# Layer 0's keys and queries of six of eight head pairs by seven block products

## The chip, the cores and the metric

The kernel runs on one core of one Trainium2 chip. The metric is the device time of one execution in microseconds. Five engines are named in what follows: TensorE (PE, matrix multiplications, with its weight loads shown apart as PEld), VectorE (DVE), ScalarE (ACT), GpSimd (POOL) and SyncE (SP, which here only issues transfers). They run side by side, each through its own list of instructions, and wait for one another through semaphores.

## The reference

Everything is in float32. The input x has 2 batches of 512 channels by 64 x 32 = 2048 tokens. Two layers follow one another.

Layer 0 is a softmax attention with 8 heads of 64. The queries and keys see 64 more channels than the values: an embedding of the row and of the column of a token, the same in both batches.

```python
qk_hs = jnp.concatenate([hidden_states, emb], axis=1)    # 512 + 64 channels
q = qk_hs @ Wq
k = qk_hs @ Wk
v = v_hs @ Wv                                            # 512 channels
scores = jnp.einsum('bhqd,bhkd->bhqk', q, k) * scale
o = jnp.einsum('bhqk,bhkd->bhqd', softmax(scores), v)
return o @ Wout + bout + hidden_states
```

Layer 1 normalises, runs a Nyström attention with 256 landmarks, an iterated pseudo-inverse and a convolution of 33 taps over the values, and then a feed-forward block, whose 4-bit weights are unpacked and composed into one 512 x 512 map. Nothing of layer 1 is changed here, but two of its parts are made during layer 0, as told below.

## The kernel before

**Tiles.** Channels lie on the 128 partitions in four chunks (`KC`), tokens in four blocks of 512 (`TB`, `NTB`). Heads are taken in pairs, so a pair's keys are one tile of 128 x 2048, and there are 2 batches x 4 = 8 pairs, written (b, hp). Names ending in `_f` belong to layer 0.

**Making a pair** (`Heads0`, L861). Its work is a Python generator, `units()`, which issues one unit of instructions each time it is advanced. For the queries and for the keys it first makes the embedding terms `e` of the pair, 128 x 2048: in batch 0 one small matmul (`fp`, L889), a copy (`ft`, L891) and one broadcast addition of a row part and a column part (L894; on DVE for the first pair, on POOL for the next three), and then a store to memory (L900). Batch 1 loads what batch 0 stored (L886). Then `project` (L903) takes one block of 512 tokens per unit: four matmuls 128 x 512, one for each chunk of channels, into a PSUM bank (L907), and one DVE addition of bank and `e` into `k` or `q` (L910). Values are another four units, each of sixteen matmuls 128 x 128 and an ACT copy (L955, L962). Two maxima (L943) end the pair. `bank` hands out one of two PSUM banks. All three weight matrices of layer 0 are loaded whole at the start and stay.

**Attention of a pair** (`attention0`, L1063). 64 steps, four blocks of 512 queries by sixteen tiles of 128 keys, are issued in groups of two. A group issues its scores (L1075), the exponentials on ACT (L1083), their running addition into `acc` on DVE (L1093), and the value products of the group before (L1105). Then it may advance the *filler*, the units of the pair that comes next:

```python
            elif due - done >= 2:
                done += advance(filler, min(due - done, 3))
            if beside and i // GROUP % 8 in (1, 3, 5):
                advance(beside)
```

So a filler step has two or three units, and stands every three to five groups. `beside` is the making of the feed-forward map: DVE unpacks the 4-bit weights (L1169, L1170), a few operations per advance, and PE multiplies at its end. At the end of a query block follow the row sums `rs` (L781), a reciprocal on DVE (L1120), eight small transfers on SP that spread it over partitions (L792), and a multiplication on POOL (L1123).

**Order.** All of layer 0 is written out by the loop at L1806: while the attention of pair n runs, pair n+1 is made. The first pair is made alone at the start. During the attention of (1,0), one unit after every group, stands also `finish0_units`, the output projection of batch 0 (`yp`, L970), its residual (L977), and the statistics of the normalisation (`mean_n` L992, `xn_f` L993, `var_n` L1008); pair (1,1), made there, gets its queries only when the projection is through. Each engine works through its list in the order written. There is no planner.

**Layer 1** already makes its keys and queries by seven block products: `Combined` (L1217) forms differences of token blocks (`t_first`, `t_second`, L1232), `combine_w` those of the weights (L1296), `product` (L1873) issues two matmuls of 128 x 512, and additions from PSUM (L1883) put the blocks together. One bank, `pu`, accumulates over several products and is read in between.

Of the kernel before, what the change touches and what calls it, by code (L numbers as in the profile page):

```python
# [10 lines left out]
F32 = mybir.dt.float32  # L11
I32 = mybir.dt.int32
AF = mybir.ActivationFunctionType
ALU = mybir.AluOpType
AX = mybir.AxisListType

P = 128
B, C, H, W = 2, 512, 64, 32
# [647 lines left out]
def fast_path(  # L666
# [63 lines left out]
    def chunked(ap):  # L730
        return ap.rearrange("(k p) n -> p k n", p=P)

    def bank(name):
        return ps.tile([P, 512], F32, tag="pp", name=name)
# [74 lines left out]
    def drain(gen):  # L809
        for _ in gen:  # L810
            pass

    def gap(n=1):
        for _ in range(n):
            yield GAP
# [7 lines left out]
    emb_sb = wpool0.tile([64, H + W], F32, name="emb_f")  # L823
    nc.vector.memset(emb_sb[:32, H:], 0.0)
    nc.vector.memset(emb_sb[32:, :H], 0.0)
    w_sb = {kind: wpool0.tile([P, KC, C], F32, name=f"w{kind}_f") for kind in "qk"}
    we = {kind: wpool0.tile([64, C], F32, name=f"we{kind}_f") for kind in "qk"}

    def load_w0(kind, cols, queue=nc.sync):
        w = {"q": wq0, "k": wk0}[kind]  # L830
        queue.dma_start(w_sb[kind][:, :, cols], chunked(w[:C, cols]))
        queue.dma_start(we[kind][:, cols], w[C:, cols])

    load_w0("q", slice(0, P), nc.scalar)
    nc.scalar.dma_start(emb_sb[:32, :H], freq)
    nc.scalar.dma_start(emb_sb[32:, H:], time)

# [11 lines left out]
    warm = bank("warm")  # L849
    for i in range(20):  # L850
        nc.tensor.matmul(warm[:, :P], lhsT=mean_w, rhs=mean_w, start=True, stop=True)
    load_w0("k", slice(0, P))
    xbs += load_x(x, 0, "x0", 1, NTB - 1)
    wv_sb = wpool0.tile([P, KC, C], F32, name="wv_f")
    nc.sync.dma_start(wv_sb[:, :, :P], chunked(wv0[:, :P]))
    nc.sync.dma_start(wv_sb[:, :, P:], chunked(wv0[:, P:]))
    for kind in "qk":
        load_w0(kind, slice(P, C))
    nc.sync.dma_start(b0_sb, b0)

    class Heads0:  # L861


        def __init__(self, b, hp, xbs):
            self.b, self.hp, self.xbs = b, hp, xbs
            self.name = f"f0_{b}_{hp}"
            self.n_units = 13 if b else 15

        def begin(self):
            self.cols = slice(self.hp * P, (self.hp + 1) * P)  # L870
            self.k = kvpool.tile([P, S], F32, tag="k", name=f"k_{self.name}")
            self.v = kvpool.tile([P, NST, P], F32, tag="v", name=f"v_{self.name}")

        def embedded_and_projected(self, kind):

            cols, xbs = self.cols, self.xbs
            if kind == "q":
                self.q = qopool.tile([P, S], F32, tag="qo", name=f"q_{self.name}")

            def embedded(kind):  # L880


                e = wpool0.tile([P, H, W], F32, tag="e", name=f"e_{kind}_{self.name}")
                flat, kept = e.rearrange("p h w -> p (h w)"), e_d["qk".index(kind), self.hp]
                if self.b:
                    nc.sync.dma_start(flat, kept)  # L886
                    return flat
                fp = bank(f"fp_{kind}_{self.name}")
                nc.tensor.matmul(fp[:, : H + W], lhsT=we[kind][:, cols], rhs=emb_sb, start=True, stop=True)  # L889
                ft = wpool0.tile([P, H + W], F32, tag="ft", name=f"ft_{kind}_{self.name}")  # L890
                nc.vector.tensor_copy(ft, fp[:, : H + W])  # L891

                engine = nc.gpsimd if self.b or self.hp else nc.vector
                engine.tensor_tensor(  # L894
                    e,
                    ft[:, :H].unsqueeze(2).to_broadcast([P, H, W]),
                    ft[:, H:].unsqueeze(1).to_broadcast([P, H, W]),
                    ALU.add,
                )
                nc.sync.dma_start(kept, flat)  # L900
                return flat

            def project(kind, dst, e, t):  # L903
                toks = slice(t * TB, (t + 1) * TB)
                pp = bank(f"pp_{kind}_{self.name}_{t}")
                for k in range(KC):
                    nc.tensor.matmul(  # L907
                        pp, lhsT=w_sb[kind][:, k, cols], rhs=xbs[t][:, k, :], start=k == 0, stop=k == KC - 1
                    )
                nc.vector.tensor_tensor(dst[:, toks], pp, e[:, toks], ALU.add)  # L910

            dst = self.q if kind == "q" else self.k
            e = embedded(kind)
            if self.b:
                yield from gap(2)
            else:
                yield
                yield GAP
            for t in range(NTB):
                project(kind, dst, e, t)  # L920
                yield

        def values(self):
            for t in range(NTB):
                values_of_tokens(self.v, t, self.xbs[t], lambda k: wv_sb[:, k, self.cols], self.name)
                yield

        def units(self, queries_first=True, ready=None, wait=0):

            self.begin()  # L930
            yield from gap(wait)
            if queries_first:
                yield from self.embedded_and_projected("q")
            yield from self.embedded_and_projected("k")
            yield from self.values()
            if not queries_first:
                while not ready():
                    yield GAP
                yield from self.embedded_and_projected("q")

            big = small.tile([P, 2], F32, tag="big0", name=f"big_{self.name}")
            for i, m in enumerate((self.q, self.k)):
                nc.vector.tensor_reduce(big[:, i : i + 1], m, AX.X, ALU.max, apply_absolute_value=True)  # L943
            i = self.b * NPAIR + self.hp
            nc.vector.scalar_tensor_tensor(
                bound[:, i : i + 1], big[:, :1], D**-0.5, big[:, 1:], ALU.mult, ALU.mult
            )
            yield
# [114 lines left out]
    def attention0(hd, filler, n_filler, needed, beside=None, every=False):  # L1063
# [58 lines left out]
            spread(rinv, few)  # L1122
            nc.gpsimd.tensor_tensor(o, o, rinv, ALU.mult)  # L1123

        pending, done = [], 0
        for i in range(0, len(steps) + 1, GROUP):
            group = [(step, scores(*step)) for step in steps[i : i + GROUP]]
            for step, p in group:
                add(step, p)
            for step, p, its_acc in pending:  # L1130
                values(step, p, its_acc)
            pending = [(step, p, acc) for step, p in group]
            due = n_filler * (i + GROUP) // len(steps)
            if every:
                done += advance(filler, 2 if due - done >= 2 else 1)
            elif due - done >= 2:
                done += advance(filler, min(due - done, 3))
            if beside and i // GROUP % 8 in (1, 3, 5):
                advance(beside)
            if not group:  # L1140
                while needed in filler:
                    advance(filler)
            if late:
                sums(*late)
                late = None
# [658 lines left out]


    todo = [(b, hp) for b in range(B) for hp in range(NPAIR)]  # L1806
    cur = Heads0(0, 0, xbs)
    drain(cur.units())
    ffn_map = [feed_forward_map()]
    oTs, finish, work = [], None, []  # L1810
    for n, (b, hp) in enumerate(todo[:-1]):
        nb, nhp = todo[n + 1]
        if nb != b:
            xbs = load_x(x, nb, "x0")
        nxt = Heads0(nb, nhp, xbs)
        n_fill = nxt.n_units + 2 * len(work)
        if finish is None:
            units = nxt.units(wait=nb - b)
        else:

            units = nxt.units(False, lambda: outs_done)
            work.append(finish)
            n_fill += N_FINISH0
        work.append(units)
        attention0(cur, work, n_fill, units, ffn_map if finish is None else None, finish is not None)
        finish = None
        oTs.append(cur.q)
        if n == 3:
            while ffn_map:
                advance(ffn_map)  # L1830
            wo_sb = load_wo(wo0, "wo_f0")
            write_bands()
        if hp == NPAIR - 1:
            outs_done = []
            finish = finish0_units(b, oTs, outs_done)
            oTs = []
        cur = nxt
# [16 lines left out]
    class Unit:  # L1854
# [15 lines left out]
        def product(self, to, m, start=True):  # L1870
            w, x = self.pair.ws[m], self.part.of[m]
            for k in range(2):
                nc.tensor.matmul(  # L1873
                    to, lhsT=w[:, k, :], rhs=x[:, k, :], start=start and k == 0, stop=k == 1, skip_group_check=True
                )
# [586 lines left out]
```

## Time and profile before

| | |
|---|---|
| median of 3 runs | 2720.01 us (2719.69 to 2721.13) |
| the profiled execution | 2717.38 us, of which the span of the core's work is 2715.6 |
| mean granted PE clock | 0.998 of full |
| PE busy | 2669.3 us, 98% of the span |
| PE weight loads (beside the matmuls) | 1353.2 us, 50% |
| DVE busy | 1676.7 us, 62% |
| ACT busy | 905.5 us, 33% |
| POOL busy | 161.4 us, 6% |
| layer 0's part | about the first half of the span |

Busy time is the time in which an engine executes; an engine that waits for a semaphore is idle, and the trace names who released it. Line numbers are those of the kernel's file. In the groups of the page, a name with `_f` is layer 0's, and the columns are busy time, mean duration of one instruction, and the idle time just before such instructions.

### The profile page before, as it was taken

How to read it: one execution, taken by the hardware profiler on the slowest of the kernel's cores; microseconds unless marked ns; L12 is line 12 of the kernel's file. 1: busy time of each engine (PE TensorE's matmuls, PEld its weight loads, DVE VectorE, ACT ScalarE, POOL GpSimd, SP SyncE). 2: the span in 40 equal slices, each digit the busy share in tenths (PEclk: the TensorE clock that was granted, in tenths of full speed). 3: DMA queues.
4: the chain of work that ended last, by engine and by line, in shares of the span. 5: the costliest groups of instructions: out<-in, count | busy, mean ns of one | idle time of the engine just before them, and what ended most of it. 6: DMA issues, size and time to landing. Idle time of an engine off the chain costs nothing.

```text
span 2715.6 us, 41051 instructions
## 1 busy us (share of the span) xinstructions
PE 2669.3 (98%) x16946; PEld 1353.2 (50%) x16946; DVE 1676.7 (62%) x2115; ACT 905.5 (33%) x1354; POOL 161.4 (6%) x109
## 2 busy tenths in 40 slices
PE   9999999999999999999999899999999999999998
PEld 5343343434443334344344455777677666655344
DVE  3768777674657765656668865535644645465565
ACT  1434344433334334444422323223323223231210
POOL 0101011000001100000001000000000000000000
PEclk9999999999999999999999999999999999999999
DMA  4100000212111300012015632313111113021211
GB/s 148 43 10 24 24 24 24 85 37 70 32 51 58 110 23 22 24 40 77 21 43 180 240 115 102 107 34 107 63 38 62 59 44 101 31 74 39 90 39 48
DMA packets 108021, 174.00 MB, mean 64 GB/s; under 512 B 15792, under 2 KB 67504, under 8 KB 103216
## 3 DMA queue, kind: packets, MB, share of 16 engines
q1 hardware_dynamic: 101680, 150.00, 16.9%
q0 software_dynamic: 5440, 20.97, 2.1%
q8 instruction: 135, 2.21, 0.3%
q14 instruction: 62, 0.51, 0.1%
q10 hardware_dynamic: 704, 0.31, 0.0%
HBM read 90.87 MB, written 63.57 MB: 57 GB/s over the span
## 4 chain that ended last, share of the span: by engine, by line
PE 90%; DVE 6%; ACT 1%; DMA 1%; SPq 1%; issue 1%; POOL 0%; DVEq 0%; ACTq 0%; POOLq 0%
PE sc_f L1075 15%; PE av_f L1105 15%; PE pa L1624 5%; PE pb L1624 5%; PE vp_f L955 4%; PE vp L955 4%; PE pp_k_f L907 4%; PE fp_g L1780 4%; PE yp_g L970 4%; PE yp_f L970 3%; PE pp_q_f L907 3%; PE pu L1873 3%; PE sc L1453 2%; PE sc L1681 2%; PE av L1474 2%; PE pp L1275 2%
## 5 line engine op out<-in xcount | busy, mean ns | idle before, releaser
L1093 DVE TENSOR_TENSOR acc_f<-acc_f,p_f 128x1024 f32<-128x1024 f32 x448 | 582.3, 1300 | 208.7 <-ACT p_f L1083 180.1
L1083 ACT ACTIVATE p_f<-sc_f 128x1024 f32<-128x1024 f32 x512 | 496.4, 1021 | 564.2 <-PE sc_f L1075 561.5
L1075 PE MATMUL sc_f<-q_f,k_f 64*64 64x512 f32 x4096 | 491.1, 594 | 2.7 <-ACT p_f L1083 2.7
L1105 PE MATMUL av_f<-p_f,v_f 64*64 64x512 f32 x4096 | 484.3, 589 | 0.0
L1105 PEld LDWEIGHTS av_f<-p_f,v_f 64*64 64x64 f32 x4096 | 156.5, 133 | 283.1 <-issue 283.1
L1075 PEld LDWEIGHTS sc_f<-q_f,k_f 64*64 64x64 f32 x4096 | 145.8, 133 | 285.7 <-issue 262.0
L1624 PE MATMUL pa<-M 128*128 128x192 f32 (+1 forms) x640 | 152.6, 383 | 5.5 <-ACT M L1615 5.5
L1624 PE MATMUL pb<-R 128*128 128x192 f32 (+1 forms) x640 | 149.3, 380 | 0.0
L1624 PEld LDWEIGHTS pa<-M 128*128 128x128 f32 x640 | 109.0, 195 | 27.0 <-ACT M L1615 8.6
L955 PEld LDWEIGHTS vp_f<-wv_f,x 128*128 128x128 f32 x1024 | 115.7, 192 | 13.5 <-issue 11.8
L955 PE MATMUL vp_f<-wv_f,x 128*128 128x128 f32 x1024 | 118.7, 277 | 0.0
L1624 PEld LDWEIGHTS pb<-R 128*128 128x128 f32 x640 | 106.5, 190 | 23.1 <-DVE M L1637 0.3
L907 PE MATMUL pp_k_f<-x,wk_f 128*128 128x512 f32 x256 | 114.3, 599 | 1.4 <-DVE k_f L910 1.0
L907 PE MATMUL pp_q_f<-x,wq_f 128*128 128x512 f32 x256 | 114.2, 598 | 0.9 <-DVE q_f L910 0.5
L970 PE MATMUL yp_f<-q_f,wo_f 128*128 128x512 f32 x256 | 114.2, 597 | 0.7 <-DVE xr_f L977 0.7
L970 PE MATMUL yp_g<-o,wo_f 128*128 128x512 f32 x256 | 114.8, 597 | 0.0
L1123 POOL TENSOR_TENSOR q_f<-q_f,rinv_f 128x512 f32<-128x512 f32 x32 | 45.9, 1436 | 1042.7 <-DMA rinv_f<-acc_f 807.7
L955 PE MATMUL vp<-w,xh 128*128 128x128 f32 x896 | 105.9, 277 | 0.0
L955 PEld LDWEIGHTS vp<-w,xh 128*128 128x128 f32 x896 | 102.1, 192 | 4.9 <-issue 3.0
L1780 PE MATMUL fp_g<-xn_g,mT 128*128 128x512 f32 (+1 forms) x232 | 99.8, 580 | 0.0
L1686 ACT ACTIVATE p<-sc 128x512 f32<-128x512 f32 x128 | 66.6, 602 | 93.4 <-PE sc L1681 93.2
L1637 DVE SCALAR_TENSOR_TENSOR M<-M,pb 128x320 f32<-128x320 f32 (+1 forms) x160 | 60.1, 417 | 60.7 <-PE pb L1624 60.7
(252 smaller groups left out, 2979.2 us busy)
## 6 DMA issues: line engine op xcount, KB each, us to landing
xh<-xh_fd SPq DMA_DIRECT2D x12, 1024.0 KB, 5.6
rinv_f<-acc_f SPq DMA_DIRECT2D x256, 32.0 KB, 1.9
xr_f<-in_x_dram SPq DMA_DIRECT2D x8, 1024.0 KB, 5.0
x_fd<-xr_f POOLq DMA_DIRECT2D x8, 1024.0 KB, 5.2
xh_fd<-xn_f POOLq DMA_DIRECT2D x8, 1024.0 KB, 4.6
k<-k_fd SPq DMA_DIRECT2D x8, 1024.0 KB, 5.6
rinv<-acc SPq DMA_DIRECT2D x256, 32.0 KB, 1.8
x<-in_x_dram SPq DMA_DIRECT2D x7, 1024.0 KB, 5.4
```

Source lines behind the costliest of these rows:

```text
L907: nc.tensor.matmul(pp, lhsT=w_sb[kind][:, k, cols], rhs=xbs[t][:, k, :], start=k == 0, stop=k == KC - 1)
L955: nc.tensor.matmul(vp[:, j * P : (j + 1) * P], lhsT=xb[:, k, j * P : (j + 1) * P], rhs=w_of(k), start=k == 0, stop=k == KC - 1,)
L970: nc.tensor.matmul(yp, lhsT=wo_sb[:, k, m * P : (m + 1) * P], rhs=oTs[k][:, toks], start=k == 0, stop=k == NPAIR - 1,)
L1075: nc.tensor.matmul(sc[r * D : (r + 1) * D, h, :], lhsT=hd.k[rows, lo : lo + D], rhs=hd.q[rows, t * TB : (t + 1) * TB], start=True, stop=True,)
L1083: nc.scalar.activation(p, sc, AF.Exp, scale=D**-0.5)
L1093: nc.vector.tensor_tensor(acc, first if c == 1 else acc, p, ALU.add)
L1105: nc.tensor.matmul(av[r][half, :], lhsT=hd.v[keys, c, half], rhs=pp[keys, h, :], start=c == 0, stop=c == NST - 1,)
L1624: nc.tensor.matmul(dst, lhsT=lhsT[:, k, t * P : (t + 1) * P], rhs=rhs[:, k, :], start=k == 0, stop=k == 1)
L1637: nc.vector.scalar_tensor_tensor(out, m, scale, pr, ALU.mult, ALU.subtract)
L1686: nc.scalar.activation(p[:, h, :], sc, AF.Exp, scale=D**-0.5)
L1780: nc.tensor.matmul(fp[:, cols], lhsT=mT[:, k, m * P : (m + 1) * P], rhs=self.xn[:, k, cols], start=k == 0, stop=k == KC - 1,)
L1873: nc.tensor.matmul(to, lhsT=w[:, k, :], rhs=x[:, k, :], start=start and k == 0, stop=k == 1, skip_group_check=True)
```

## The change

Six of the eight pairs, all but (0,0) and (1,1), which are called *plain*, make keys and queries together, two token blocks at a time, by seven block products of two matmuls each where four projections of four matmuls stood. The products are issued in four units, [2, 1], [5, 6], [7, 3], [4]. Products 1, 6, 7 and 4 accumulate in one bank `pu`, which DVE reads after each of them; products 2, 5 and 3 go to the other bank, `pc`. DVE forms four differences of token blocks, 128 x 1024, per double block (one step ahead of their use), and four combinations of the weights, 128 x 256, per pair.

Weights are loaded pair by pair, one buffer for each of q, k and v, from the second pair on when the pair before has used its own. Embedding terms come in blocks of 512 tokens, four buffers, each made or loaded (`embed`) when an earlier one has been used. `beside` is advanced in the two groups after a filler step instead of at fixed groups. Pair (1,1) keeps its keys, values, queries order; pair (1,2), made during (1,1)'s attention, begins its products when the output projection of batch 0 is through.

The core of the diff (the plain path, arguments and the code of `units` for its order are cut):

```diff
-    w_sb = {kind: wpool0.tile([P, KC, C], F32, name=f"w{kind}_f") for kind in "qk"}
...
+    def load_w0(kind, b, hp, queue=nc.sync):
+
+        w, cols = {"q": wq0, "k": wk0, "v": wv0}[kind], slice(hp * P, (hp + 1) * P)
+        sb = wpool0.tile([P, KC, P], F32, tag=f"w{kind}", name=f"w{kind}_f_{b}_{hp}")
+        queue.dma_start(sb, chunked(w[:C, cols]))
...
+    class Tokens:
...
+            self.of = {1: x0[:, lo, :], 2: x0[:, hi, :], 3: x1[:, hi, :]}
+
+        def sum(self, m):
...
+            out = self.of[m] = wpool0.tile([P, 2, TB], F32, tag=f"t{m}", name=f"t{m}_{self.name}")
+            a, b = {
+                5: lambda: (x1[:, lo, :], x0[:, lo, :]),
+                6: lambda: (x1[:, hi, :], self.of[5]),
+                7: lambda: (x1[:, hi, :], x1[:, lo, :]),
+                4: lambda: (x0[:, hi, :], self.of[6]),
+            }[m]()
+            nc.vector.tensor_tensor(out, a, b, ALU.subtract)
...
+        def combine_w(self):
...
+            self.ws = {**blocks_of(wk, wq), 5: s1, 6: s2, 7: s3, 3: s4}
+            nc.vector.tensor_tensor(s1, wq[:, lo, :], wq[:, hi, :], ALU.add)
+            nc.vector.tensor_tensor(s2, s1, wk[:, lo, :], ALU.subtract)
+            nc.vector.tensor_tensor(s3, wk[:, lo, :], wq[:, lo, :], ALU.subtract)
+            nc.vector.tensor_tensor(s4, wk[:, hi, :], s2, ALU.subtract)
+
+        def products(self, tp, part, after):
...
+            pc = other(2)
+            begin("k", 0, pc)
+            pu = bank(f"pu_{name}")
+            product(pu, 1)
+            add("k", 0, pu)
+            part.sum(7)
+            yield
+            pc = other(5)
+            begin("k", 1, pc)
+            begin("q", 1, pc)
+            product(pu, 6, False)
+            add("k", 1, pu)
+            part.sum(4)
+            yield
+            product(pu, 7, False)
+            add("q", 1, pu)
+            pc = other(3)
+            add("k", 1, pc)
+            if after:
+                after.sum(5)
+            yield
+            product(pu, 4, False)
+            begin("q", 0, pu)
+            if after:
+                after.sum(6)
+            yield
...
+                for tp in range(2):
+                    yield from self.products(tp, parts[tp], parts[1] if tp == 0 else after)
+            if self.next:
+                self.next.load()
+                if self.next.b:
+                    self.next.embed(4)
+            for _ in values:
+                if self.next and not self.next.plain and not self.next.ws:
+                    self.next.combine_w()
                 yield
...
             due = n_filler * (i + GROUP) // len(steps)
+            since += 1
             if every:
                 done += advance(filler, 2 if due - done >= 2 else 1)
             elif due - done >= 2:
                 done += advance(filler, min(due - done, 3))
-            if beside and i // GROUP % 8 in (1, 3, 5):
+                since = 0
+            if beside and done > 1 and since in (1, 2):
                 advance(beside)
```

Here `begin(kind, t, bank)` is a DVE addition of the bank and the embedding term into the key or query block, followed by `embed()`, and `add` a DVE addition of the bank onto that block. `other(m)` takes a bank and issues product m into it.

## The prediction

> **What bounds the kernel now.** I read the page first: busy times (engine, busy us, share of the span), then the chain of waits.
>
> ```profile
> span 2715.6 us, 41051 instructions
> PE 2669.3 (98%) x16946; PEld 1353.2 (50%) x16946; DVE 1676.7 (62%) x2115; ACT 905.5 (33%) x1354; POOL 161.4 (6%) x109
> PE 90%; DVE 6%; ACT 1%; DMA 1%; SPq 1%; issue 1%; POOL 0%; DVEq 0%; ACTq 0%; POOLq 0%
> ```
>
> TensorE (PE) works 98% of the span and carries 90% of the chain, so an instruction taken from it shortens the time unless a wait takes its place. Next the costly groups and, grouped by form, the vector engine (DVE) rows that the change uses: line, engine, names, count | busy us, mean ns | idle before.
>
> ```profile
> L1093 DVE TENSOR_TENSOR acc_f<-acc_f,p_f 128x1024 f32<-128x1024 f32 x448 | 582.3, 1300 | 208.7 <-ACT p_f L1083 180.1
> L907 PE MATMUL pp_k_f<-x,wk_f 128*128 128x512 f32 x256 | 114.3, 599 | 1.4 <-DVE k_f L910 1.0
> L907 PE MATMUL pp_q_f<-x,wq_f 128*128 128x512 f32 x256 | 114.2, 598 | 0.9 <-DVE q_f L910 0.5
> ```
> ```profile
> L910 DVE TENSOR_TENSOR k_f<-pp_k_f,e_k_f 128x512 f32<-128x512 f32 x32 | 22.0, 690 | 73.6 <-PE pp_k_f L907 73.5
> L1232 DVE TENSOR_TENSOR t_first<-xh,t_first 128x1024 f32<-128x1024 f32 x4 | 7.0, 1754 | 0.0
> L1232 DVE TENSOR_TENSOR t_second<-xh,t_second 128x1024 f32<-128x1024 f32 x4 | 4.9, 1216 | 0.0
> L1296 DVE TENSOR_TENSOR s<-s,w 128x256 f32<-128x256 f32 x6 | 4.7, 777 | 0.1
> L1296 DVE TENSOR_TENSOR s<-w,s 128x256 f32<-128x256 f32 x6 | 2.5, 417 | 0.0
> ```
>
> The loops issue 8 pairs x 4 blocks x 4 matmuls = 128 for the keys; the row has 256, so one f32 matmul is two instructions. The mean of 599 ns counts overlapping ones; the real price is busy over count, 114.3/256 = 0.446 us, or the spacing in the timeline. There (start, length, engine) the attention and one filler step of two projections look so:
>
> ```profile
> 310.87 1.90 PE L1105 MATMUL av_f<-p_f,v_f 64*64 64x512 f32 x16
> 312.69 7.13 PE L907 MATMUL pp_k_f<-x,wk_f 128*128 128x512 f32 x16
> 311.69 2.55 DVE L1093 TENSOR_TENSOR acc_f<-acc_f,p_f 128x1024 f32<-128x1024 f32 x2
> 316.43 0.69 DVE L910 TENSOR_TENSOR k_f<-pp_k_f,e_k_f 128x512 f32<-128x512 f32 x1 [2.19 <-PE pp_k_f L907]
> 1585.11 1.88 PE L1873 MATMUL pu<-t_second,w_first 128*128 128x512 f32 x4
> 1586.82 1.88 PE L1873 MATMUL pu<-xh,w 128*128 128x512 f32 x4
> ```
>
> The last two are layer 1's block products, four instructions each, 1.72 us apart: 0.43 us per instruction. An attention group of two steps takes 3.43 us on PE (score starts 302.28, 305.72, 309.15); its two DVE adds take 2.6. DVE reads a finished projection 0.31 us after its last slot (312.69 + 8 x 0.43 = 316.12, then 316.43). Two stretches of layer 0 show the room (width, then busy PE, PEld, DVE):
>
> ```profile
> 276.00:400.00 124.00, 122.53 (x994) 52.45 (x987) 92.21 (x98) 52.57 (x57) 13.32 (x5) 1.00 0.06 18
> 400.00:530.00 130.00, 128.81 (x1017) 54.98 (x1020) 92.35 (x106) 52.58 (x57) 8.77 (x4) 1.00 0.18 64
> ```
>
> PE is full, DVE at 71 to 74%. PE's waits (total, times, longest) that the change touches are small:
>
> ```profile
> PE rs_f L781 <- DVE acc_f L1093: 3.0, 3, 1.2
> PE mean_n L992 <- DVE xn_f L989: 1.4, 1, 1.4
> PE pp_k_f L907 <- DVE k_f L910: 1.0, 1, 1.0
> ```
>
> [...] the trace has 0.69, 1.21 to 1.22 and 2.29, but also 1.30 (L1093) and 1.75 (t_first): up to half more. [...] layer 1 reads its running pu between products that start 1.72 us apart. [...] I price PE by starts, and a token sum issued ahead of an addition delays it.
>
> **The change, part by part.**
> *Matmuls removed.* Six of eight pairs have two double blocks each. Before, one took 2 kinds x 2 blocks x 4 = 16 matmuls; now seven products of 2 = 14. So 6 x 2 x 2 = 24 matmuls, 48 instructions: 48 x 0.43 = **-20.6 us** (-21.4 at 0.446). Scores, values, output projection and few-terms keep their counts.
> *DVE work added.* 48 token sums 128x1024 at 1.22 = 58.6 (84 at 1.754); L910's 64 additions become 112: 48 x 0.69 = 33.1; 24 weight sums 128x256 at 0.417 = 10.0 (18.6 at 0.777); the first pair's terms 8 x 0.69 for 2 x 2.29, +0.9. In all +103, DVE about 1779 us. It costs only where PE then waits. A regular step A is pc2, pu1, pc5, pu6, 16 instructions = 6.87 us of PE, with its group 10.3; DVE in it: adds 2.6, five additions 3.45, two sums 2.44 = 8.5. Step B is pu7, pc3, pu4, 5.15 us, with its group 8.6; DVE 2.6 + 2.07 + 2.44 = 7.1. Both leave room. In A, counted from pc2's start: key addition 0 reads pc2 at 2.03 to 2.72 (pc5 needs the bank at 3.43); reads pu at 3.74 to 4.43 (pu6 at 5.15). In B: queries read pu at 2.03 to 2.72 (pu4 at 3.43). Spare is 0.7 us at each of the three hand-offs, so zero wait. In front of them DVE may be behind: the map of the feed-forward runs on DVE in the two groups after a step, 2 x 2 x (0.42 + 0.69) = 4.4 us, and a block end adds 0.69 + 1.75 = 2.4. Against these 6.9 stand 4 to 5 groups of 0.83 us spare and step A's own 1.8: 5.1 to 5.9. Behind by 1.0 to 1.8 at most; B tolerates 0.7 (idle ahead of the read) + 0.7. So at most 0.35 us, two steps in three pairs: 0 to 2.1.
> *Uneven steps.* While (1,2) is built, during (1,1)'s attention, units pair up shifted: pc5, pu6, pu7, pc3 stand in one step, twice. pu7 must wait until key addition 1 has read pu: it is queued behind two additions and ends about 1.07 us after pu6's last slot. Behind pu7 stand pc3 and the next group's scores. +2.1 (0 to 4).
> *Terms in 512-token blocks.* POOL does 24 of 128x512 for 6 of 128x2048 at 4.2 to 4.5, one quarter each; no row shows the small form, 1.1 to 1.5 us each by the 128x512 multiply at 1.44. They are made steps ahead, POOL is 6% busy, and the cover is the attention group. 64 transfers of 256 KB replace 16 of 1 MB. At the start this removes DVE's 4.9 us wait for a 1 MB store, behind which PE waited 1.0 + 0.4: -1.4 (0 to -3).
> *Weights pair by pair.* 24 loads of 256 KB (the layer-1 form lands in 3.2 us) for 3 MB at once: 3 MB more in all, on a DMA that is 6 to 18% busy in these stretches. SP issues a load when the last product of the old pair has read the buffer; behind it stand the next terms and, later, the 256 small spreads of the row sums. Loads are asked at least one step, over 15 us, ahead of use, except (1,3)'s queries' weights after a lone pu4, whose weight sums land behind further value matmuls. Taken as 0; 0 to +3.2 each for the six later pairs if that cover is gone, and below nothing too, by up to 1 for the lighter start.
> *Moved.* Map steps leave the groups at block ends: half of rs_f's 3.0 goes, -1.5 (0 to -3; map steps late elsewhere are the +2.1 above). While (1,1) is built, three of its query projections now come between xn_f's subtraction and mean_n: -1.4. What is late next is the variance, in the following step, one group later.
> *Unforeseen.* The shifted steps and the map backlog: +1 to +2, I take +2 with the 0 to 2.1 above inside it.
> Sum: -20.6 -1.4 -1.5 -1.4 +2.1 +2.0 = **-20.8**. The profiled run took 2717.4 (span 2715.6), so 2696.6; the median 2720.0 stands 2.6 above it: **2699 us**.
>
> **Rivals.** 0.2%, 5.4 us, is about what a measurement of this kernel can tell from no change.
> 1. *Part of the gain goes to DVE.* Sums at 1.754 add 25 us to DVE, and stretches as above go from 92 to 92 + 17 (8 sums, 8 additions, 4 weight sums) = 109, with the dear sums 114, of about 127 us: 86 to 90%. For: DVE is in order, sums stand ahead of additions. Against: no hand-off misses its 0.7 even with dear sums. If half of the 24 steps wait 0.7: +8.4, 2707.
> 2. *Slower: the hand-offs bind.* One mechanism: DVE enters every step over 1.4 us late, so that pc5, pu6 and pu4 each wait for the read of their bank. Fully exposed that is 1.07 us at 3 x 12 = 36 places, +38.5, less the 0.0 assumed: 2737. It decides against the change from (20.8 + 5.4)/36 = 0.73 us per place. For: up to 90% occupancy, at which a late start is caught up slowly. Against: the timings of A and B above; layer 1 does the same with 0.3 to 2.8 us of such waits in all.
> 3. *Transfers late.* Weights asked late: 6 x 3.2 = +19, 2718, no change. Against: the share of DMA and the lead.
> 4. *It does not do it:* the products save no PE time since PE is paced otherwise. Against: 98% busy. 2720.
>
> **How the numbers follow.** Likeliest case 0.76 (own range 2693 to 2705: no stalls and 21.4 removed, or all small prices at their dear ends), rival 1 0.13 (2703 to 2713), rivals 3 and 4 0.05, rival 2 0.06. The range takes the first and most of rival 1: 2693 to 2711. Faster by over 0.2% (under 2714.6) 0.89, same 0.05, slower (over 2725.4) 0.06.
>
> **What the profile after would show.** Right: 336 product instructions and 128 plain ones at 0.43 us; PE busy about 2649; PE idle before products under 5 us, most of it on pu behind the key addition; token sums at 1.2; DVE about 1779 us; no PE wait on weights; mean_n gone from the waits. Wrong: token sums at 1.75 with idle before pc or pu in every pair (rivals 1, 2); DVE waiting for w transfers, with sc waiting for p behind it (rival 3); PE busy unchanged (4). The forecast itself is wrong outside 2693 to 2711.

## The result, and the profile after

The changed kernel takes **2706.11 us** in the median (2704.39 to 2707.50, 6 runs) against 2719.85 (2717.86 to 2722.65, 6 runs) for the kernel before: a ratio of 0.9949 with a 95% interval of 0.9936 to 0.9962, so 13.7 us or 0.5% faster. The forecast was 2699, 20.8 us faster, with a range of 2693 to 2711. The profiled executions are 2705.95 and 2717.38 us.

The head of the page after, to be laid beside the lines of before (busy us, share, instructions):

```profile
span 2704.1 us, 41287 instructions
PE 2653.0 (98%) x16898; PEld 1347.4 (50%) x16898; DVE 1760.5 (65%) x2241; ACT 907.9 (34%) x1356; POOL 179.3 (7%) x127
PE 87%; DVE 9%; ACT 1%; issue 1%; DMA 1%; SPq 1%; DVEq 0%; ACTq 0%
```

PE has 48 instructions fewer (16946 to 16898) and 16.3 us less to do: 18.1 less in layer 0 and 1.7 more in layer 1, where its instructions are the same. DVE has 84 us more. The chain's share of DVE rose from 6 to 9% and PE's fell from 90 to 87%: waits for DVE took some of what the matmuls gave. The waits of PE name them (total, times, longest):

```profile
PE pc_f L979 <- DVE k_f L994: 3.0, 3, 1.7
PE pu_f L979 <- DVE q_f L999: 2.1, 3, 0.9
PE rs_f L781 <- DVE acc_f L1243: 2.0, 2, 1.4
PE pp_q_f L952 <- DMA x<-in_x_dram: 1.9, 1, 1.9
PE var_n L1158 <- DVE xr_f L1155: 1.6, 1, 1.6
PE pu_f L979 <- DVE k_f L999: 1.6, 2, 0.8
PE pu_f L979 <- ACT rstd_n L1160: 0.4, 1, 0.4
```

Four rows concern the products (`pc_f` and `pu_f`), together 7.1 us. Since a matmul's modelled end lies 0.16 us behind its slot (0.59 against 0.43), nine such waits cost 8.4 us when counted from start to start. The rows of the products and of the new DVE work, by form, read:

```profile
L979 PE MATMUL pc_f<-t,s_f 128*128 128x512 f32 x48 | 23.1, 603 | 3.0 <-DVE k_f L994 3.0
L979 PE MATMUL pu_f<-t,wq_f 128*128 128x512 f32 x96 | 47.0, 612 | 3.6 <-DVE q_f L999 2.1 <-DVE k_f L999 1.6
L887 DVE TENSOR_TENSOR t<-x,t 128x1024 f32<-128x1024 f32 x24 | 31.6, 1318 | 0.1
L887 DVE TENSOR_TENSOR t<-x 128x1024 f32<-128x1024 f32 x12 | 16.3, 1357 | 0.0
L887 DVE TENSOR_TENSOR t<-x,x 128x1024 f32<-128x1024 f32 x12 | 14.6, 1214 | 0.0
L1243 DVE TENSOR_TENSOR acc_f<-acc_f,p_f 128x1024 f32<-128x1024 f32 x448 | 572.5, 1278 | 197.1 <-ACT p_f L1233 166.6 <-DVE acc_f L1243 1.4
L999 DVE TENSOR_TENSOR k_f<-pu_f,k_f 128x512 f32<-128x512 f32 x24 | 16.6, 691 | 12.4 <-PE pu_f L979 12.0
```

The durations are those of the forecast: 0.69 us for an addition, 1.21 to 1.36 for a token sum. So no single operation was slow enough to explain the waits; what stood ahead of them has to be looked at.

**Where, pair by pair.** The starts of the first scores of each attention cut layer 0 into stages; the trace gives their lengths in us. The last column is the time between start and start of the product steps beyond 0.43 us.

| stage | before | after | difference | product waits after |
|---|---|---|---|---|
| first pair, alone | 52.6 | 52.3 | -0.3 | |
| attention (0,0), making (0,1) | 159.0 | 155.3 | -3.7 | 0.4 |
| (0,1), making (0,2) | 159.6 | 157.8 | -1.8 | 2.9 |
| (0,2), making (0,3) | 159.6 | 158.3 | -1.3 | 2.7 |
| (0,3), making (1,0) | 172.7 | 169.2 | -3.5 | 0 |
| (1,0), making (1,1), plain | 226.3 | 225.9 | -0.4 | |
| (1,1), making (1,2) | 157.5 | 159.7 | +2.2 | 2.4 |
| (1,2), making (1,3) | 156.9 | 153.8 | -3.1 | 0 |

Eight instructions at 0.43 are 3.4 us a pair: the two pairs without waits give about that (3.5 and 3.1), and the three with waits over 2 us give less. In (1,1)'s attention there stand, beside the product waits, a row sum that waits 1.4 us and the last `var_n`, which came one stage earlier in the kernel before. Layer 0 is counted here up to the start of the last score, 1375.8 us before and 1363.9 after, so -11.9 us. Layer 1, whose code is the same, took 1332.1 and 1331.8 us from there to its last matmul, and the kernel's last stores 0.8 more after than before. So layer 0 carries the difference of the profiles.

What put DVE behind at the first product step of (0,2)'s making is in the timeline of DVE after (start, length, operation):

```profile
208.75 0.69 DVE L1314 TENSOR_TENSOR tmp_f<-tmp_f,hits_f 128x512 f32<-128x512 f32 x1
...
210.27 0.68 DVE L1262 TENSOR_TENSOR q_f<-av_f,q_f 128x512 f32<-128x512 f32 x1
210.88 2.27 DVE L1093 TENSOR_REDUCE big_f<-q_f 128x1 f32<-128x2048 f32 x1
213.07 2.28 DVE L1093 TENSOR_REDUCE big_f<-k_f 128x1 f32<-128x2048 f32 x1
215.38 0.16 DVE L1095 SCALAR_TENSOR_TENSOR bound<-big_f 128x1 f32<-128x1 f32 x1
215.45 1.75 DVE L1270 RECIPROCAL acc_f<-rs_f 128x256 f32<-128x256 f32 x1
217.12 1.16 DVE L1243 TENSOR_TENSOR acc_f<-p_f,p_f 128x1024 f32<-128x1024 f32 x1
218.39 11.41 DVE L1243 TENSOR_TENSOR acc_f<-acc_f,p_f 128x1024 f32<-128x1024 f32 x8
...
230.05 7.17 DVE L1243 TENSOR_TENSOR acc_f<-acc_f,p_f 128x1024 f32<-128x1024 f32 x4
237.14 0.68 DVE L994 TENSOR_TENSOR k_f<-pc_f,e_k_f 128x512 f32<-128x512 f32 x1
```

A map step, the two maxima of the finished pair and a reciprocal stand at the turn of the pairs. From then on DVE is idle hardly at all until 237: the additions of six groups follow one another. The first key addition could have read pc2 (product 2 in its bank pc) 2.03 us after that product's start at 232.52. It starts at 237.14, that is 4.6 us after the start of pc2, and 2.6 later than it could. The last four additions ahead of it took 7.17 us, 1.79 each where the mean is 1.28: POOL was making embedding terms just then.

```profile
230.28 3.88 POOL L940 TENSOR_TENSOR e_k_f<-ft_k_f 128x512 f32<-128x512 f32 x2 [4.22 <-DVE ft_k_f L923]
234.12 4.01 POOL L940 TENSOR_TENSOR e_q_f<-ft_q_f 128x512 f32<-128x512 f32 x2
```

From 231.4 us on additions and terms start by turns, one of each about every 2.0 us: an addition takes 1.88 us there and a term 2.02, where at other places they take 1.22 and 1.04. In the whole trace the 425 additions into `acc` with no tensor operation of POOL beside them took 1.22 us in the mean and 1.23 at most, the 55 beside one 1.68 in the mean. The four additions together are 2.0 us longer than at the mean. No run takes POOL's terms away, so this part is read from the trace and not tested. Meanwhile pc5, the next product for the other bank, needs the bank that holds pc2:

```profile
234.34 1.88 PE L979 MATMUL pu_f<-x,wk_f 128*128 128x512 f32 x4
237.88 1.98 PE L979 MATMUL pc_f<-t,s_f 128*128 128x512 f32 x4 [1.66 <-DVE k_f L994]
```

### The profile page after: what moved, and what is told of

It is laid out like the page before. It is cut to its first block, busy times and chain, and to the rows that moved or that the text cites. A ratio compares the mean times of both kernels' runs of the same rounds, so it can differ in the third digit from the quotient of the medians.

```text
span 2704.1 us, 41287 instructions
## 1 busy us (share of the span) xinstructions
PE 2653.0 (98%) x16898; PEld 1347.4 (50%) x16898; DVE 1760.5 (65%) x2241; ACT 907.9 (34%) x1356; POOL 179.3 (7%) x127
## 4 chain that ended last, share of the span: by engine, by line
PE 87%; DVE 9%; ACT 1%; issue 1%; DMA 1%; SPq 1%; DVEq 0%; ACTq 0%
PE sc_f L1225 14%; PE av_f L1255 14%; PE pa L1776 5%; PE pb L1776 5%; PE vp_f L1105 4%; PE vp L1105 4%; PE fp_g L1932 4%; PE yp_g L1120 4%; PE yp_f L1120 4%; DVE acc_f L1243 3%; PE pu_f L979 3%; PE pu L2042 3%; PE sc L1605 2%; PE sc L1833 2%; PE av L1626 2%; PE pp L1427 2%
## 5 line engine op out<-in xcount | busy, mean ns | idle before, releaser
L1243 DVE TENSOR_TENSOR acc_f<-acc_f,p_f 128x1024 f32<-128x1024 f32 x448 | 572.5, 1278 | 197.1 <-ACT p_f L1233 166.6
L1870 POOL TENSOR_TENSOR o<-o,rinv 128x512 f32<-128x512 f32 x32 | 46.1, 1442 | 815.1 <-DVE rinv L1869 621.5
L1789 DVE SCALAR_TENSOR_TENSOR R<-M,pa 128x320 f32<-128x320 f32 (+1 forms) x160 | 58.5, 407 | 49.3 <-PE pa L1776 49.2
```

The costliest lines, as they stand in the source:

```text
L1243: nc.vector.tensor_tensor(acc, first if c == 1 else acc, p, ALU.add)
L1789: nc.vector.scalar_tensor_tensor(out, m, scale, pr, ALU.mult, ALU.subtract)
```

## The experiments

The theory: each removed instruction is worth its 0.43 us, and what is missing of the gain are waits at hand-offs that DVE reaches late, because of work at the pairs' ends and of the map, not because of the token sums. All diffs are against the changed kernel. Ratios are to the kernel before.

**1. All eight pairs plain**

```diff
-            self.plain = (b, hp) in ((0, 0), (1, 1))
+            self.plain = True
```

> All eight pairs by plain projections, with the pair-by-pair weights, the 512-token terms and the new places of the map steps kept. Theory (the saving of the matmuls is the forecast 20.6 to 21.4 us, and the shortfall is waits plus clock): 48 PE instructions come back, +21, and the product waits (8.4 us) and the late row sum (1.6) go: 2716 to 2719 us, PE busy about 2669 to 2674, that is 1 to 4 us under the kernel before. Rival A (a product instruction saves much less than 0.43 us, because the PE time is paced otherwise): no more than 2712. Rival B (the loading and the blocks of terms cost time): over 2722. If the longer stretches at half PE clock come with the denser PE work of the products, the mean clock is back at 0.998 here; if they are the chip's own, it stays at 0.996 to 0.997.

Measured: 2722.14 us, ratio 1.0008 (0.9999 to 1.0016), a profiled span of 2720.0. So the loading pair by pair, the blocks of terms and the moved map gain nothing by themselves and may cost up to 0.16%; the seven products are worth 16.0 us of median. In the traces layer 0 goes from 1378.1 (plain) to 1363.9, that is -14.2; the products' waits add 8.4, the row sums wait 2.2 less. Then 20.4 us are left for the 48 instructions, 0.425 each (0.44 if the 0.8 us by which the first pair, the same in both, was longer in the changed kernel's profile is counted too): the forecast's price holds. The time is 3 us over what was expected. Layer 0 is 2.3 us longer than in the kernel before, where the theory had a small gain: rival B, the cost of loading and order, holds in this size, and its threshold of 2722 is just reached. The stage that grew is (1,1)'s attention, +3.2 us: its last row sum waits 1.9 us for additions behind the pair's end, and the last `var_n` moved into it. The first pair is 1.1 us shorter.

```profile
PE rs_f L781 <- DVE acc_f L1243: 4.3, 4, 1.9
```

The mean clock stayed at 0.996 to 0.997 without the products, as it is with them, so they are not what sets it.

**2. Without fifteen of the sixteen levels of the map**

```diff
-                if i and level:
+                if False:
```

> Leaves out the unpacking of fifteen of the sixteen levels of the 4-bit weights (56 pairs of DVE operations, 62 us of DVE), so the map is not the reference's; all else as in the changed kernel. Theory (the waits of the products in the first three pairs come from DVE being behind, through map steps and the work at the end of a pair, the two maxima above all): the six waits there fall from 6.0 us to 1 to 3, those after the pair's end (1.8 and 1.3) shrinking least; 2701 to 2703 us. Rival (the token sums in front of the additions are the cause): waits stay at 5 to 6 us, 2705 to 2707.

Measured: 2702.94 us, ratio 0.9934 (0.9921 to 0.9948), as the theory had it. DVE has 54 us less to do, not 62. Of the products' 7.1 us in PE's waits 3.9 are left, and in the first three pairs only those behind a pair's end:

```profile
PE pc_f L979 <- DVE k_f L994: 1.9, 2, 1.7
PE pu_f L979 <- DVE k_f L999: 1.6, 2, 0.8
```

The waits on the query addition (2.1) are gone: they were the map's. The 1.7 in the first product step of (0,2)'s making is unmoved: that one is not. The one in the first step of (0,3)'s making fell from 1.1 to 0.2 us, so there the map had a part. The row with `k_f` L999 is the uneven steps of (1,2), where no map runs.

**3. Without the token sums**

```diff
-            out = self.of[m] = wpool0.tile([P, 2, TB], F32, tag=f"t{m}", name=f"t{m}_{self.name}")
...
-            nc.vector.tensor_tensor(out, a, b, ALU.subtract)
+            self.of[m] = {5: x1[:, lo, :], 6: x1[:, hi, :], 7: x1[:, hi, :], 4: x0[:, hi, :]}[m]
```

> Leaves out the 48 differences of token blocks (the products read plain token blocks, so keys and queries are not the reference's). Theory: the waits of pc on the first key addition (1.8, 1.3, 0.4) stay mostly, since no sum of the own step stands ahead of it, while the two of pu4 in the second half of a pair (1.06 each) go; product waits fall from 8.4 to about 5, the uneven steps keep 1.9 of it; 2702 to 2704 us. Rival (sums are the cause): product waits under 2.5 us in all, 2698 to 2700.

Measured: 2703.97 us, ratio 0.9947 (0.9934 to 0.9961). 58 us of DVE are gone, and of the products' 7.1 us of waits 6.6 remain:

```profile
PE pc_f L972 <- DVE k_f L987: 2.8, 2, 1.7
PE pu_f L972 <- DVE q_f L992: 1.8, 2, 0.9
PE pu_f L972 <- DVE k_f L992: 1.6, 2, 0.8
```

The sums are not the cause, more clearly than the theory had it: it gave them the waits on the query addition, and these stayed too (1.8 of 2.1). What the sums did cost is a row sum's wait in (1,1)'s attention: 1.4 us with them, 0.3 without.

**4. Steps of (1,2) aligned, the map at fixed groups**

```diff
+                if (self.b, self.hp) == (1, 2):
+                    next(values)
+                    yield
...
-            if beside and done > 1 and since in (1, 2):
+            if beside and i // GROUP in (12, 13, 17, 18, 21, 22, 23, 25, 26, 27, 29, 30):
```

> Whole computation. Two moves: one value unit of pair (1,2) is issued ahead of its products, so that its steps are [2,1,5,6] and [7,3,4] as in the other pairs; and the map advances at twelve fixed groups of each attention (12, 13, 17, 18, 21 to 23, 25 to 27, 29, 30), away from the first product step and the last group of a pair. Theory: the uneven steps' 1.9 goes, most of the 6.0 us beside the map goes (1 to 2 us left), the row sum that waited 1.6 us behind them shrinks: 2697 to 2700 us. Rival (the waits come back at other hand-offs, since DVE has the same work in the same stretch): 2703 to 2706.

Measured: 2702.57 us, ratio 0.9944 (0.9930 to 0.9957); the gain was expected about twice as large.

```profile
PE rs_f L781 <- DVE acc_f L1246: 2.3, 3, 0.9
PE pc_f L979 <- DVE k_f L994: 1.5, 1, 1.5
PE pu_f L979 <- DVE q_f L999: 1.4, 2, 0.9
```

The stage of (1,1) shrank from 159.7 to 156.4 us, with no product wait left in it. But the map's waits partly moved: (0,3)'s attention, which had none, now had a pc wait of 1.5 and a pu wait, since its product steps stand at other groups (9, 14, 19, 24). Of the row sums' 2.3 us, 1.5 follow the last map step of an attention; the other 0.8 are in (1,1)'s attention, where no map runs.

**5. The two maxima right after the last product**

```diff
+            big = small.tile([P, 2], F32, tag="big0", name=f"big_{self.name}")
+            for i, m in enumerate((self.q, self.k)):
+                nc.vector.tensor_reduce(big[:, i : i + 1], m, AX.X, ALU.max, apply_absolute_value=True)
...
             if self.next:
                 self.next.load()
...
-            big = small.tile([P, 2], F32, tag="big0", name=f"big_{self.name}")
-            for i, m in enumerate((self.q, self.k)):
-                nc.vector.tensor_reduce(big[:, i : i + 1], m, AX.X, ALU.max, apply_absolute_value=True)
...
             yield
```

> Whole computation. The two maxima that end a pair (4.6 us of DVE) are issued right after its last product (or projection of keys or queries) instead of after its last value unit; the map's places are those of the changed kernel. Theory (at group 6 of an attention DVE is still behind from the pair's end: maxima 4.6, reciprocal 1.7): the waits of pc on the first key addition, 1.8 and 1.3 us, fall under 0.5 each; the two of pu4 at group 20 stay; 2702 to 2704 us. Rival (it is the map step at group 5 alone): they stay, 2705 to 2707.

Measured: 2704.00 us, ratio 0.9938 (0.9924 to 0.9951). PE's wait on the first key addition fell from 3.0 us in three places to one of 0.2; that on the query addition is the same as in the changed kernel:

```profile
PE pu_f L979 <- DVE q_f L999: 2.1, 3, 0.9
PE pc_f L979 <- DVE k_f L994: 0.2, 1, 0.2
```

So the waits in the first product step need the maxima at the pair's turn (in (0,3)'s making maxima and map together, since without either the wait nearly goes), and those in the later steps are the map's.

**6. All three together, the map where value units stand**

```diff
+            if beside and (hd.b, hd.hp) == (0, 3):
+                if done > 1 and since in (1, 2):
+                    advance(beside)
+            elif beside:
+                advance(beside, (2, 12, 13, 17, 21, 25, 25, 26, 27, 29, 29).count(i // GROUP))
```

with the aligned steps of 4 and the early maxima of 5.

> Whole computation. The maxima early, the value unit of pair (1,2) ahead of its products, and the map in the first three attentions at groups 2, 12, 13, 17, 21, 25 (twice), 26, 27, 29 (twice), where DVE has room because value units stand there or a product step is over; in the fourth as in the changed kernel, where no product waited. Theory: of 8.4 us of product waits under 2 are left, row sums wait under 1.5 in all: 2697 to 2700 us. Rival (DVE's work in these stretches is what counts, not its place): 2703 or more.

Measured: **2696.32 us** (2694.19 to 2699.99), ratio 0.9912 (0.9898 to 0.9925), better than both kernels. One product wait is left, and one row sum:

```profile
PE rs_f L781 <- DVE acc_f L1246: 0.8, 1, 0.8
PE pc_f L979 <- DVE k_f L994: 0.2, 1, 0.2
```

DVE is as busy (1768 us) as in the changed kernel (1760): only the places differ. Layer 0 is 11.0 us shorter than the changed kernel's, 1352.9 against 1363.9. At the same place as above DVE is idle for 0.6 and 0.9 us at the start of the attention, and the first key addition starts 2.6 us after its pc2, although the last four additions are as slow beside POOL as before:

```profile
231.15 1.98 PE L979 MATMUL pc_f<-x,wk_f 128*128 128x512 f32 x4
```
```profile
226.69 7.17 DVE L1246 TENSOR_TENSOR acc_f<-acc_f,p_f 128x1024 f32<-128x1024 f32 x4
233.78 0.68 DVE L994 TENSOR_TENSOR k_f<-pc_f,e_k_f 128x512 f32<-128x512 f32 x1
```

**7. Every token sum twice**

```diff
             nc.vector.tensor_tensor(out, a, b, ALU.subtract)
+            nc.vector.tensor_tensor(out, a, b, ALU.subtract)
```

> Every difference of token blocks is formed twice (48 more of 1.22 us, 59 us of DVE), the result is the same. This prices DVE work at the hand-offs. Theory (DVE catches up between steps except beside the map and behind a pair's end): waits grow by 2 to 7 us, 2708 to 2713. Rival (the hand-offs bind in every step): each of 24 steps is late by the 2.4 us of its two more sums, less the spare 0.7 to 1.4: +25 to +40, 2730 or more.

Measured: 2726.90 us, ratio 1.0027 (1.0017 to 1.0038), 20.8 over the changed kernel and slower than the kernel before: a miss of the theory, and short of its rival. In the trace layer 0 grew by 15.3 us: 13.8 in the three pairs made beside the map (4.0, 4.9, 4.9) and 2.1 in the other three, for about 29 us of added DVE work in each half. Product waits rose to 13.7 and row sums waited for their additions:

```profile
PE pc_f L980 <- DVE k_f L995: 8.3, 5, 2.6
PE rs_f L781 <- DVE acc_f L1244: 8.3, 7, 2.7
```

The theory took the spare between two steps as enough to catch up; beside the map there was nearly none, and half of what is added comes through. The profiled execution is the shortest of the eight (2722.02 us, up to 2731.28), 16.1 over the changed kernel's; what makes the others longer this run does not show.

**8. The map at its old places**

```diff
-            if beside and done > 1 and since in (1, 2):
+            if beside and i // GROUP % 8 in (1, 3, 5):
```

> The map advances at groups 1, 3 and 5 of each eight as in the kernel before; all else as in the changed kernel. Theory: three map steps (6.6 us of DVE) now stand between a pair's end and the first product step at group 6, and one each ahead of the steps at 11 and 20: product waits of the first three pairs rise from 6.0 to 10 to 15 us and row sums wait longer; 2710 to 2716. Rival (the place of the map does not matter to the products): 2705 to 2708.

Measured: 2719.16 us, ratio 0.9997 (0.9988 to 1.0005), beyond the theory's 2710 to 2716. The line that looks like housekeeping in the diff decides over the whole gain. Three map steps now stand between the turn of the pairs and the first product step. The timeline of PE, and windows around it (busy PE, PEld, DVE, ACT, POOL, then the granted clock, DMA share and GB/s):

```profile
234.98 1.88 PE L979 MATMUL pu_f<-x,wk_f 128*128 128x512 f32 x4
242.96 3.78 PE L979 MATMUL pc_f<-t,s_f 128*128 128x512 f32 x4 [6.10 <-DVE k_f L994]
246.54 2.76 PE L979 MATMUL pu_f<-t,s_f 128*128 128x512 f32 x4
```
```profile
235.00:242.00 7.00, 1.86 (x5) 0.55 (x3) 6.83 (x7) 0.00 (x0) 3.83 (x3) 0.96 0.40 150
242.00:249.00 7.00, 6.04 (x8) 2.41 (x8) 4.30 (x6) 0.00 (x0) 2.43 (x3) 0.55 0.10 37
```

pc5 waits 6.1 us, and the matmuls after it run at half speed, 3.78 us instead of 1.98. The same happens one pair later. Product waits are 18.5 us in all, most of them on the first key addition; the row sums wait 1.4 us, no longer than in the changed kernel.

```profile
PE pc_f L979 <- DVE k_f L994: 14.4, 5, 6.1
```

The theory had no slower clock in it: in the two stretches at half speed the matmuls of the product steps lose another 3.1 and 2.0 us against 0.43 each.

## Why the prediction was right, and where it was off

The direction and the stated range held, and so did the mechanism of the gain, PE time saved for each matmul taken away. The likeliest case did not hold: 2706 lies outside its own range of 2693 to 2705 and where rival 1 was put, so the stated range held because most of rival 1 was inside it. Of the signs written down for the profile, PE idle before products is 7.1 us where under 5 stood. The step that was mis-sized is "Unforeseen" with the map backlog, 0 to 2.1 us where 6.0 were measured. In the forecast's terms, in layer 0:

- *Matmuls removed:* -20.6 forecast; -20.4 by experiment 1. Right in size.
- *DVE work added:* +103 us forecast, +84 in the page (the running additions into `acc` took 10 us less than before, 572.5 for 582.3), +96 against the plain kernel. The durations were right, 0.69 us for 512 elements of a partition and 1.21 to 1.36 for 1024. That it costs nothing by itself held only where nothing else is in front: pairs (1,0) and (1,3) have no product wait at all.
- *The backlog ahead of a step:* 0 to 2.1 us forecast, taken inside +2.0; 6.0 measured in the first three pairs, plus 0.6 in (1,1)'s attention, where pu waits for its bank behind the normalisation's square root. The sum 6.9 against 5.1 to 5.9 was set up for the end of a query block. It left out the end of a pair, where two maxima (4.6 us) come on top: the working never asked what the reductions of L943 would be ahead of. About 3 of the 6.0 us go with the maxima (experiment 5), and about 3 are in the later steps and go with the map (experiment 2), where at most 2.1 had been put. It also left out that DVE's additions are slower beside POOL, 2.0 us at one such place; this is read from the trace alone.
- *Uneven steps:* +2.1 forecast, two waits of 0.95 from start to start measured, 1.9 us. Right; experiment 4 removes them. The row sum that waits 1.4 us in the same attention was in no term.
- *Map steps moved:* -1.5 forecast for the row sums, -0.7 to -0.9 measured. The larger effect was not in the working: that the old places would have stalled the products (experiment 8, 13 us).
- *mean_n:* -1.4 forecast and gone, but "late next is the variance" was left without a price: `var_n` waits 1.6. Together +0.2.
- *Start:* -1.4 forecast, -0.3 measured: DVE's wait for a store shrank from 4.9 to 3.5 us and PE's wait behind it at pp_k is gone, while a projection waited 1.9 us for x. In the experiments, which start alike, that wait is 0.5 to 1.3 us in seven and absent in experiment 3, so part of it is chance.
- *Weights and terms:* taken as 0. Loads landed in 2.8 to 3.0 us in the median and no matmul waited for one; DVE waited once, 1.1 us. The small POOL form took 1.35 us (keys) and 1.76 (queries) in the mean, the second more than the 1.1 to 1.5 estimated, and no wait names it; beside it DVE's additions were slower (1.88 us for 1.22 at the place shown above).

The sum of these: 8.4 of product waits where 4.1 stood, and about 0.9 us gained at row sums, statistics and start where 4.3 stood, is 7.7 of the 8.9 us by which layer 0 missed the forecast; 1.2 us are not assigned. By medians the shortfall is 7.1. Experiment 1 cuts the same 8.9 us otherwise: with it as the base, the products brought -14.2 where -16.5 was forecast (-20.6, +2.1, +2.0), and all the rest of the change +2.3 where -4.3 was forecast. The two cuts differ because row sums wait 4.3 us in experiment 1 and 2.0 in the changed kernel: part of the waiting may only change its place. So the terms that were forecast as gains beside the products are a part of the miss too, and how much of it is theirs is not one number.

Of the rivals, the first had the amount (8.4 us, 2707) and half the place. That its 8.4 is the 8.4 of the trace is chance. It put the lateness on dear sums, and half of all steps late; without sums it stays, and it sits in three pairs and the uneven steps. The second did not happen, but experiments 7 and 8 show it is real: some 20 us of product and row-sum waits were enough to take the whole gain.

## What to carry to other kernels

When an engine at 65% gets a hand-off inside a step of the engine at 98%, its mean share says little: add up what stands in its queue in the groups before that hand-off, above all at the seams of the loop (end of a pair, end of a block), and compare it with the spare of these groups. The same work at another place was worth 10 us here (experiment 6), and 13 the other way (experiment 8). Price a moved side job by what it will be ahead of, not only by what it stops delaying.

## What the runs showed of the hardware

In these traces the granted PE clock was half at a few places, each with an idle gap of PE in or just ahead of its beginning. In experiment 8, 6.1 us of idle ended at 242.96, with half speed from 241.5 to 248.3, and it came again in the next pair (0.50 from 408 to 412). Each of the two kernels has two such stretches in layer 1: the kernel before from 2419.9 and 2505.2 us on, 3.4 us each, with gaps of 2.06 and 4.11 us; the changed kernel from 1483.4 and 2490.4 us on, 6.8 us each, with gaps of 2.53 and 4.15. One more stands behind the last matmul of each. Within a run the beginnings of the two differ by a whole multiple of 3.413 us, the length of the shorter ones: 85.3 us in the kernel before (25 times), 1006.9 in the changed kernel (295 times). None of the eight gaps of 1.5 to 1.7 us in the two kernels was followed by one, and not every longer one was: the kernel before had gaps of 2.24, 2.24 and 2.53 us without, the changed kernel 2.06 and 2.24. The gap of 2.53 us is that of the same `sc` instructions in both, and so is that of 2.06 of `wp`: each had a stretch in one kernel and none in the other. What decides is not shown. The stretches fell at different places of the same instructions from run to run: layer 1 took from 1331.8 us (the changed kernel) to 1337.1 (experiment 5), more than a third of the change itself, and laid matmul by matmul beside one another, the traces of the two kernels drift apart by more than 0.4 us only in or just behind such stretches. So the stall of 6.1 us in experiment 8 cost 3.1 us on top of its own length, and the last few us of a comparison are better read by stages of the trace than by the span.
